# Layer 2's weights by way of copies in DRAM, landed raw in their own places and split later

## The chip, the cores and the metric

The kernel runs on one core of a Trainium2 chip. The metric is the device time of one execution in microseconds. In the text PE is TensorE (PEld its weight loads), DVE VectorE, ACT ScalarE, POOL GpSimd and SP SyncE, which here only issues DMAs.

## The reference

Two cross-attention layers run one after the other over x (16 batches, 256 queries, 320 channels) and a context (16 batches, 256 tokens, 512 channels). H is 20 heads of D = 16.

```python
def layer0(x, ctx):               # 77 text tokens, 179 image tokens
    text, ip = ctx[:, :77], ctx[:, 77:]
    q, k, v = heads(x @ Wq), heads(text @ Wk), heads(text @ Wv)
    text_out = softmax(q k^T * scale) v
    q_sem = softmax(x @ Wq @ (text @ Wk)^T * scale) @ text
    sem   = (q_sem @ ip^T) * scale                      # one for all heads
    ip_probs = softmax(q heads(ip @ Wk_ip)^T * scale + 0.5 * sem) * spatial_mask
    return (text_out + ip_probs heads(ip @ Wv_ip)) @ Wout + bout + x

def layer1(x, ctx):               # 252 text tokens, 4 image tokens
    text, ip = ctx[:, :-4], ctx[:, -4:]
    probs = softmax(q k^T * scale);  text_out = probs v
    sem   = l2norm(probs @ text) @ l2norm(ip)^T         # per head
    ip_probs = softmax(q heads(ip @ Wk_ip)^T * scale + 0.5 * sem) * spatial_mask
    return (text_out + ip_probs heads(ip @ Wv_ip)) @ Wout + bout + x

x = layer0(x, ctx); return layer1(x, ctx)
```

Each layer has six weights: Wq, Wk, Wk_ip, Wv, Wv_ip and Wout. In the kernel those of the first layer are `wq0`, `wk0`, `wki0`, `wv0`, `wvi0`, `wo0`, and those of the second, which the texts call layer 2, `wq1`, `wk1` and so on.

## The kernel before

The work goes in slots, one for four heads of one batch: 80 slots for the first layer (`slot0`), 80 for the second (`slot1`). Within a slot of the first layer `score0` forms the scores of the slot after the next on PE and their maxima on DVE (L676, L677); `maxima0` turns the maxima and ACT sends them as small rows (`qs<-mt`, L687) into Q; `turned0` forms the scores again the other way round (L699), ACT takes the exponential (L702) and POOL multiplies (L705); `attend0` applies the values (L732) and `settle0` transposes and normalizes on DVE (`nt` L743, `tmp` L749). `stacks` loads the K, Q, T (`tph`) and M tiles of the slot four ahead from DRAM by SP.

Everything else is a task with a list of due times in slots: keys, values and queries of coming batches, the closing projection of finished ones, and the preparation of layer 2's weights. `fill(now)` runs what is due at three points of a slot. The order on PE is the order in which the program calls; the other engines' order is set when the program is built, by a planner, except for instructions tied by `queued` (it stands behind the last `anchor` of its engine).

Matrix products run in a format that rounds, so each operand is kept as two halves: `halves` makes the high half by a rounding copy on ACT (L147) and the low half by a subtraction on DVE (L148). A weight's tile holds both, `w[:, 0]` high and `w[:, 1]` low. `in_turn` loads a weight part by part into the two-buffer ring `rawc` and splits each part out of it; a part's load is issued as the part before last is split, and a buffer is taken again only when its split is done. `weights` does this by rows, `weights_by_column` in three column blocks into the `wB` tiles.

Layer 2's weights take the places of layer 1's: `wB` (wki, later wvi), `wA` (wk), `wC` (wv), `wE` (wq), `wF` (wo). The tasks are `weights1` (due from slot 59: the image tokens, their norms, `cip`), `weights7` (from 62: wki, three products for the image keys, wk), `weights6` (from 67: wv, wvi, three products for the image values), `weights2` (from 71.6: wq) and `weights4` (wo; at 2.6 for layer 1, from slot 84 for layer 2). The first keys of layer 2 are due at slot 73.

## Time and profile before

| | |
|---|---|
| median of 3 runs | 1620.4 us (1616.49 to 1623.62) |
| the profiled execution | 1612.52 us |
| its span, first to last instruction | 1610.7 us |
| granted TensorE clock, mean | 0.977 |
| busy share: PE, PEld, DVE, ACT, POOL | 94, 76, 75, 53, 74% |

The profile is of one execution, with each instruction's start and duration. A view of stretches gives each engine's busy time in a piece of the span; a view of waits names the waiting engine and line, and after the arrow what ended the wait, with the sum, the count and the longest. A timeline row has start, duration, engine, line and operation, output and input tiles, and in brackets the idle time of the engine just before, with what ended it.

### The profile page before, as it was taken

What the parts mean: (1) busy time and instruction counts of PE and PEld (TensorE: products, weight loads), DVE (VectorE), ACT (ScalarE), POOL (GpSimd) and SP (SyncE); (2) the same over time, 40 slices, a digit from 0 to 9 for tenths busy, and PEclk for the clock granted to TensorE, in tenths of its full rate; (3) what the DMA queues carried; (4) which work ended last, traced back from release to release, by engine and by line L of the source; (5) the groups of instructions that cost most, each with busy time, mean ns of one, the idle gap of its engine ahead of it and who ended that gap; (6) DMA issues with size and microseconds to landing.
All of it is one profiled execution on the core that took longest, in us unless ns stands there. A gap on an engine that the chain in (4) does not pass through costs nothing.

```text
span 1610.7 us, 36262 instructions
## 1 busy us (share of the span) xinstructions
PE 1518.9 (94%) x13194; PEld 1218.1 (76%) x13194; DVE 1212.2 (75%) x2426; ACT 847.1 (53%) x1861; POOL 1195.7 (74%) x1227
## 2 busy tenths in 40 slices
PE   7899999999999899789999999999999999999996
PEld 6787878787878787577777777777777777777765
DVE  5466777777777678877877787778777887788785
ACT  5344545555555545446656556555655655565562
POOL 3358787878787867777688768876877787778785
PEclk9899999999999899799999999999999999999998
DMA  6767777777677576665424333433343333423301
GB/s 218 214 200 204 206 204 206 205 205 211 199 204 210 170 213 174 162 198 177 149 67 133 114 127 96 131 119 120 96 136 121 107 109 127 130 90 104 110 27 45
DMA packets 235741, 243.05 MB, mean 151 GB/s; under 512 B 19050, under 2 KB 219468, under 8 KB 235564
## 3 DMA queue, kind: packets, MB, share of 16 engines
q1 hardware_dynamic: 233356, 239.44, 49.7%
q8 instruction: 105, 1.72, 0.4%
q10 hardware_dynamic: 2208, 1.30, 0.3%
q14 instruction: 72, 0.59, 0.1%
HBM read 116.78 MB, written 88.18 MB: 127 GB/s over the span
## 4 chain that ended last, share of the span: by engine, by line
PE 63%; DMA 9%; DVE 8%; POOL 8%; ACT 4%; issue 3%; SPq 1%; ACTq 0%; POOLq 0%; DVEq 0%
PE X L205 16%; PE X L839 13%; PE X L551 7%; PE P L732 6%; PE P L848 4%; PE S L675 4%; PE T L798 3%; PE P L851 3%; PE T L699 3%; POOL wt L830 2%; DMA kd<-kst 2%; DMA qs<-qd 2%; DMA qs<-mt 2%; PE S L803 2%; DVE wt L840 1%
## 5 line engine op out<-in xcount | busy, mean ns | idle before, releaser
L705 POOL TENSOR_TENSOR P<-P,rs 128x512 f32<-128x512 f32 x320 | 413.8, 1313 | 149.6 <-ACT P L702 149.5
L830 POOL TENSOR_TENSOR wt<-P,ctb 128x512 f32<-128x512 f32 x320 | 419.0, 1324 | 95.0 <-ACT ctb L829 93.6
L839 PE MATMUL X<-ctb,gm 128*128 128x512 f32 x1120 | 329.9, 412 | 0.7 <-DVE wt L840 0.4
L702 ACT ACTIVATE P<-T 128x512 f32<-128x512 f32 x320 | 176.0, 595 | 211.8 <-PE T L699 113.9
L839 PEld LDWEIGHTS X<-ctb,gm 128*128 128x128 f32 x1120 | 188.9, 188 | 69.2 <-issue 15.2
L840 DVE TENSOR_TENSOR wt<-X,wt 128x512 f32<-128x512 f32 x320 | 218.4, 683 | 18.9 <-PE X L839 13.4
L804 DVE TENSOR_REDUCE mn<-S 128x4 fp32r<-128x1008 f32 x160 | 191.7, 1198 | 49.1 <-PE S L803 48.9
L829 ACT ACTIVATE ctb<-P 128x512 fp32r<-128x512 f32 x320 | 195.1, 630 | 40.1 <-PE X L839 35.8
L811 ACT ACTIVATE P<-T 128x512 f32<-128x512 f32 x320 | 173.1, 593 | 68.9 <-PE P L848 53.8
L677 DVE TENSOR_REDUCE mn<-S 128x4 fp32r<-128x716 f32 x160 | 142.5, 891 | 0.0
L699 PE MATMUL T<-qs,ks 127*128 127x256 f32 x640 | 111.7, 294 | 21.9 <-DVE tmp L749 9.8
L732 PE MATMUL P<-P,vr 128*32 128x256 f32 x1920 | 128.7, 404 | 0.9 <-DVE mx L604 0.9
L675 PE MATMUL S<-ks,qs 125*128 125x256 f32 x640 | 118.4, 309 | 4.9 <-DVE mn L677 2.8
L675 PEld LDWEIGHTS S<-ks,qs 125*128 125x128 f32 x640 | 89.2, 196 | 41.3 <-issue 36.2
L551 PE MATMUL X<-ho,wF 128*128 128x256 f32 x768 | 113.2, 291 | 6.5 <-DVE ho L541 3.0
L551 PE MATMUL X<-hq,wE 128*128 128x256 f32 x768 | 109.7, 286 | 7.1 <-ACT hq L540 3.2
L917 POOL TENSOR_TENSOR r<-u,rs 128x40 f32<-128x40 f32 (+2 forms) x17 | 108.7, 6394 | 7.4 <-DVE u L914 7.2
L551 PEld LDWEIGHTS X<-ho,wF 128*128 128x128 f32 x768 | 103.7, 195 | 12.7 <-DVE ho L541 4.6
L699 PEld LDWEIGHTS T<-qs,ks 127*128 127x128 f32 x640 | 92.5, 197 | 27.2 <-DVE tmp L749 11.2
L551 PEld LDWEIGHTS X<-hq,wE 128*128 128x128 f32 x768 | 102.3, 193 | 11.3 <-ACT hq L540 3.7
L205 PE MATMUL X<-cta,wA 128*128 128x252 f32 (+1 forms) x720 | 101.1, 287 | 8.9 <-ACT wA L147 5.8
L205 PEld LDWEIGHTS X<-cta,wA 128*128 128x128 f32 x720 | 94.3, 193 | 15.1 <-ACT wA L147 6.1
(207 smaller groups left out, 2854.9 us busy)
## 6 DMA issues: line engine op xcount, KB each, us to landing
qd<-q SPq DMA_DIRECT2D x96, 384.0 KB
qs<-tph SPq DMA_DIRECT2D x64, 308.0 KB
kd<-kst SPq DMA_DIRECT2D x73, 256.0 KB
rawc<-in_cT_dram SPq DMA_DIRECT2D x60, 256.0 KB
qs<-qd SPq DMA_DIRECT2D x80, 192.0 KB
ks<-kd SPq DMA_DIRECT2D x80, 192.0 KB
ks<-kd SPq DMA_DIRECT2D x160, 96.0 KB
qs<-qd SPq DMA_DIRECT2D x160, 96.0 KB
```

The source lines that it names most:

```text
L205: last = mm(out, lhs(a, k), rhs(b, k), start=i == 0, stop=i == len(terms) - 1)
L551: mm(pp, w(s, k, slice(m * 128, (m + 1) * 128)), a[:, t], start=i == 0, stop=i == len(terms) - 1)
L675: mm(sp[:, h], Q[: XROW + T0, h, t * 128 : (t + 1) * 128], K[: XROW + T0, h], start=True, stop=True)
L699: mm(st[p][:, j], K[:KS0, 2 * p + j, t * 128 : (t + 1) * 128], Q[:KS0, 2 * p + j], start=True, stop=True)
L702: exp = anchor(nc.scalar.activation(pt, st[p], AF.Exp, scale=SCALE))
L705: anchor(nc.gpsimd.tensor_mul(pt, pt, rs[:, t : t + 1].to_broadcast([128, 2, S])))
L732: mm(pv[32 * s : 32 * s + 32, o : o + S], v[:, vt, h : h + 32], P[k, s // 2][:, t, s % 2], start=vt < 2, stop=vt != 1,)
L804: anchor(nc.vector.tensor_reduce(maxes[k + 2][:, t], sp[:, :, :T1], axis=AX.X, op=ALU.max))
L829: nc.scalar.activation(R[k, u][:, t], P[k, u][:, t], AF.Copy, scale=0.5)
L830: anchor(nc.gpsimd.tensor_sub(W[k, u][:, t], P[k, u][:, t], f(R[k, u][:, t])))
L839: mm(yp, gm[:, gb], R[k, u][:, kt], start=i == 0, stop=i == len(blocks[n]) - 1)
L840: nc.vector.tensor_mul(W[k, u][:, n], yp, W[k, u][:, n])
```

## The change

The 22 row blocks of layer 2's six weights are copied from the inputs into tiles in DRAM (`aside`), one block at a time: every second slot from 14 to 48, and once a slot from 58 to 61. Each copy stands on SP's queue behind the last K load of `stacks0`, which is an anchor now. Later each weight is brought from its copy, unsplit, into the low halves of its own place, in one load (three for the column blocks), as soon as that place's last reader in layer 1 is done: the `LANDINGS`, due at slots 62, 66.6, 68 and 84. The splits then read and write in place: the high half is copied from the low one, and the low half has the high one subtracted from itself. `weights7`, `weights6` and `weights4` start a slot later than before (63, 68, 85); `weights2` stays at 71.6, with one step less. Layer 1's output weight keeps the old way under a name of its own, `first_output`.

```diff
-    def weights(w_d, tag, half=None, wait=0, raw="raw"):
-        ...
-        yield from in_turn([(w_d[k * 128 : (k + 1) * 128], w[:, 0, k], w[:, 1, k]) for k in range(kt)], wait, raw)
+    aside = {}
+
+    def set_aside():
+        for name, w_d in (("wk", wk1_d), ("wv", wv1_d), ("wvi", wvi1_d), ("wq", wq1_d), ("wo", wo1_d), ("wki", wki1_d)):
+            aside[name] = dram.tile(list(w_d.shape), F32, name=f"{name}_aside")
+            for k in range(w_d.shape[0] // 128):
+                rows = slice(k * 128, (k + 1) * 128)
+                queued(nc.sync.dma_start(aside[name][rows], w_d[rows]))
+                yield
+
+    landing = {}
+
+    def land(name, tag):
+        src = aside[name].rearrange("(k p) n -> p k n", p=128)
+        if tag == "wB":
+            parts = landing[name] = [buf("wB", [128, 2, 4, 128], FR, bufs=SIZES["WB"]) for m in range(3)]
+            for m, w in enumerate(parts):
+                queued(nc.sync.dma_start(f(w[:, 1]), src[:, :, m * 128 : (m + 1) * 128]))
+        else:
+            w = landing[name] = buf(tag, [128, 2, src.shape[1], src.shape[2] + (NIP if name == "wv" else 0)], FR)
+            queued(nc.sync.dma_start(f(w[:, 1, :, : src.shape[2]]), src))
+
+    def cast(parts):
+        for hi, lo in parts:
+            halves(hi, lo, f(lo), nc.vector, True)
+            yield
+
+    def weights(name, half=None):
+        w = landing.pop(name)
+        n = w.shape[3] - (NIP if name == "wv" else 0)
+        yield from cast([(w[:, 0, k, :n], w[:, 1, k, :n]) for k in range(w.shape[2])])
...
-    def weights_by_column(w_d, wait=0, raw="raw"):
-        ...
-        yield from in_turn([(src[:, :, m * 128 : (m + 1) * 128], w[:, 0], w[:, 1]) for m, w in enumerate(parts)], wait, raw)
+    def weights_by_column(name):
+        parts = landing.pop(name)
+        yield from cast([(w[:, 0], w[:, 1]) for w in parts])
...
             if part == "K":
-                dma(K[0:XROW], stack_rows(kd[0][b // 2][:, :, b % 2])[:, hs])
+                anchor(nc.sync.dma_start(f(K[0:XROW]), stack_rows(kd[0][b // 2][:, :, b % 2])[:, hs]))
...
+    LANDINGS = (
+        ("wki", "wB", 62, ("k0", B // 2 - 1)),
+        ("wk", "wA", 62, ("k0", B // 2 - 1)),
+        ("wv", "wC", 66.6, ("v0", B - 1)),
+        ("wvi", "wB", 66.6, ("w7",)),
+        ("wq", "wE", 68, ("q0", B - 1)),
+        ("wo", "wF", NS + 4, ("c0", B - 1)),
+    )
...
-    task(("w7",), thirds(13, 62), weights7, ("w1",), ("k0", B // 2 - 1))
-    task(("w6",), thirds(13, 67), weights6, ("w7",), ...)
-    task(("w2",), [71.6, 72, 72.2, 72.6, 73], weights2, ("q0", B - 1), ("w6",))
+    task(("w7",), thirds(13, 63), weights7, ("w1",), ("land", "wki"), ("land", "wk"))
+    task(("w6",), thirds(13, 68), weights6, ("w7",), ("land", "wv"), ("land", "wvi"), ...)
+    task(("w2",), [71.6, 72, 72.2, 72.6], weights2, ("land", "wq"), ("w6",))
...
-    task(("w4", 1), spread(NS + 4, 0.33, 4), lambda: weights4(1), ("c0", B - 1))
+    task(("w4", 0), [2.6, 2.8, 3, 3.2], first_output, ("k0", 1))
+    task(("aside",), [14 + 2 * i for i in range(18)] + [58, 59, 60, 61], set_aside)
+    for name, tag, t, *needs in LANDINGS:
+        task(("land", name), [t], lambda name=name, tag=tag: iter([land(name, tag)]), *needs)
+    task(("w4", 1), [NS + 5, NS + 5.33, NS + 5.67], weights4, ("land", "wo"))
```

More of the change, by code (lines that the diff above doesn't have):

```diff
@@ L168, in in_turn @@
                 yield
-    def weights(w_d, tag, half=None, wait=0, raw="raw"):
-        rows, n = w_d.shape
-        kt = rows // 128
-        w = buf(tag, [128, 2, kt, n], FR)
-        yield from in_turn([(w_d[k * 128 : (k + 1) * 128], w[:, 0, k], w[:, 1, k]) for k in range(kt)], wait, raw)
+    aside = {}
[6 more added lines that the diff above has]
+                yield
@@ L176, in weights @@
+    def cast(parts):
[6 more added lines that the diff above has]
+        yield from cast([(w[:, 0, k, :n], w[:, 1, k, :n]) for k in range(w.shape[2])])
         if half is not None:
             nc.vector.tensor_scalar_mul(w[:, 1, 2], f(w[:, 1, 2]), half)
+        if name == "wv":
+            w1["wv"] = w
         return lambda s, k, m=slice(None): w[:, s, k, m]
-    def weights_by_column(w_d, wait=0, raw="raw"):
-        parts = [buf("wB", [128, 2, 4, 128], FR, bufs=SIZES["WB"]) for m in range(3)]
-        src = w_d.rearrange("(k p) n -> p k n", p=128)
-        yield from in_turn([(src[:, :, m * 128 : (m + 1) * 128], w[:, 0], w[:, 1]) for m, w in enumerate(parts)], wait, raw)
+    def weights_by_column(name):
+        parts = landing.pop(name)
+        yield from cast([(w[:, 0], w[:, 1]) for w in parts])
@@ L185, in weights_by_column, with first_output @@
         return lambda s, k, m: parts[m.start // 128][:, s, k]
+    def first_output():
+        w = buf("wF", [128, 2, 3, CP], FR)
+        yield from in_turn([(wo0_d[k * 128 : (k + 1) * 128], w[:, 0, k], w[:, 1, k]) for k in range(3)], 0.1, "rawc")
+        nc.vector.tensor_scalar_mul(w[:, 1, 2], f(w[:, 1, 2]), tmask[:, 4:5])
+        wo.append(lambda s, k, m=slice(None): w[:, s, k, m])
     def all_halves(jobs, rings):
@@ L401, in weights7 @@
         cip = w1["cip"]
-        wki1 = yield from weights_by_column(wki1_d, 0.3, "rawc")
+        wki1 = yield from weights_by_column("wki")
         for m in range(3):
@@ L407, in weights7 @@
             yield
-        w1["k"] = yield from weights(wk1_d, "wA", None, 0.3, "rawc")
+        w1["k"] = yield from weights("wk")
     def weights6():
         cip = w1["cip"]
-        wv = w1["wv"] = buf("wC", [128, 2, 4, H * D + NIP], FR)
-        parts = [(wv1_d[k * 128 : (k + 1) * 128], wv[:, 0, k, : H * D], wv[:, 1, k, : H * D]) for k in range(4)]
-        yield from in_turn(parts, 0.3, "rawc")
-        wvi1 = yield from weights_by_column(wvi1_d, 0.3, "rawc")
+        w1["v"] = yield from weights("wv")
+        wvi1 = yield from weights_by_column("wvi")
         vip = buf("rawc", [128, 512], bufs=2, name="vip")[:BI, :CP]
@@ L436, in weights2, with weights4 @@
     def weights2():
-        wq.append((yield from weights(wq1_d, "wE", tmask[:, 3:4], 0.3, "rawc")))
-    def weights4(l):
-        wo.append((yield from weights((wo0_d, wo1_d)[l], "wF", tmask[:, 4:5], (0.1, 0.3)[l], "rawc")))
+        wq.append((yield from weights("wq", tmask[:, 3:4])))
+    def weights4():
+        wo.append((yield from weights("wo", tmask[:, 4:5])))
     def weights3():
@@ L1055, in xattn2 @@
     task(("w1",), thirds(7, 59), weights1)
-    task(("w7",), thirds(13, 62), weights7, ("w1",), ("k0", B // 2 - 1))
-    task(("w6",), thirds(13, 67), weights6, ("w7",), *[(x, c) for c in range(B) for x in ("v0", "m0t")])
-    task(("w2",), [71.6, 72, 72.2, 72.6, 73], weights2, ("q0", B - 1), ("w6",))
+    task(("w7",), thirds(13, 63), weights7, ("w1",), ("land", "wki"), ("land", "wk"))
+    task(("w6",), thirds(13, 68), weights6, ("w7",), ("land", "wv"), ("land", "wvi"), *[(x, c) for c in range(B) for x in ("v0", "m0t")])
+    task(("w2",), [71.6, 72, 72.2, 72.6], weights2, ("land", "wq"), ("w6",))
     for i in range(2):
         task(("w3", i), [NS - 4 + 5 * i], weights3)
-    task(("w4", 0), [2.6, 2.8, 3, 3.2], lambda: weights4(0), ("k0", 1))
-    task(("w4", 1), spread(NS + 4, 0.33, 4), lambda: weights4(1), ("c0", B - 1))
+    task(("w4", 0), [2.6, 2.8, 3, 3.2], first_output, ("k0", 1))
[3 more added lines that the diff above has]
+    task(("w4", 1), [NS + 5, NS + 5.33, NS + 5.67], weights4, ("land", "wo"))
     def stacks(k):
```

## The prediction

> **What bounds the kernel now.** I read the page's first two parts, then the busy time by stretches cut at the first exponential of a slot (L702, four to a slot), then the waits of those stretches, and last the order of time on VectorE where PE waits for it.

> ```profile
> PE 1518.9 (94%) x13194; PEld 1218.1 (76%) x13194; DVE 1212.2 (75%) x2426; ACT 847.1 (53%) x1861; POOL 1195.7 (74%) x1227
> PE   7899999999999899789999999999999999999996
> PEclk9899999999999899799999999999999999999998
> DMA  6767777777677576665424333433343333423301
> q1 hardware_dynamic: 233356, 239.44, 49.7%
> q8 instruction: 105, 1.72, 0.4%
> ```

> PE is busy 94% of the span and the kernel follows it. A slice is 40.3 us; PE falls under 9 tenths, apart from start and end, only in slices 13, 16 and 17 (523 to 725 us), where the layers overlap and layer 2's weights are brought in. There alone can this change win.

> ```profile
> core 0: us, PE busy (x) PEld busy (x) DVE busy (x) ACT busy (x) POOL busy (x), PEclk, DMA share, GB/s
> 428.90:509.10 80.20, 76.83 (x722) 66.34 (x721) 60.43 (x135) 40.66 (x94) 65.38 (x64) 1.00 0.72 206
> 541.10:554.80 13.70, 7.66 (x68) 6.41 (x67) 8.56 (x25) 5.92 (x11) 10.25 (x10) 0.80 0.85 248
> 581.90:602.20 20.30, 18.16 (x174) 15.72 (x172) 14.29 (x37) 8.46 (x23) 11.95 (x11) 1.00 0.83 240
> 602.20:633.50 31.30, 31.30 (x298) 27.62 (x298) 26.42 (x54) 18.01 (x40) 26.58 (x23) 1.00 0.54 148
> 633.50:643.20 9.70, 6.66 (x60) 5.22 (x58) 7.25 (x14) 3.58 (x9) 5.77 (x6) 0.91 0.81 231
> 643.20:658.20 15.00, 7.66 (x48) 5.29 (x48) 11.54 (x27) 5.11 (x13) 6.81 (x9) 0.61 0.64 178
> 658.20:680.70 22.50, 18.03 (x174) 13.56 (x173) 18.27 (x36) 11.48 (x22) 19.03 (x18) 0.88 0.57 145
> ```

> Rows 2 to 7 are slots 58, 62 to 63, 64 to 67, 68, 69 and 70 to 72; row 1 is ten steady slots of layer 1. Length less PE's busy time is PE's idle time: 3.4 us in the ten steady slots, then 6.0, 2.1, 0, 3.0, 7.3 and 4.5. Slot 58 waits for the image tokens, which the change leaves alone. Slots 68 to 72 together lose 14.9 us in 47.2, and in them the granted clock is low as well.

> **Where the raw loads are late.** The waits of slots 63, 68, 69 and 70 to 72, in this order:

> ```profile
> ACT wB L147 <- DMA rawc<-in_wki_dram: 4.8, 1, 4.8
> PE X L551 <- DVE M L365: 1.7, 1, 1.7
> ACT wC L147 <- DMA rawc<-in_wv_dram: 3.9, 1, 3.9
> DVE wC L148 <- ACT wC L147: 2.4, 1, 2.4
> PE X L683 <- DVE mn L677: 2.8, 1, 2.8
> PE T L699 <- DVE tmp L749: 3.9, 1, 3.9
> PE X L616 <- DVE sp L612: 3.5, 1, 3.5
> ACT wB L147 <- DMA rawc<-in_wvi_dram: 2.7, 1, 2.7
> PE X L683 <- DVE mn L677: 2.2, 2, 2.0
> PE X L683 <- DMA qs<-tph: 1.3, 1, 1.3
> SPq L82 <- DMA rawc<-in_wvi_dram: 4.8, 1, 4.8
> ```

> Three times ScalarE stands before a split whose raw weights have not landed: 4.8, 3.9 and 2.7 us. What PE pays is less. The 4.8 us cost it nothing: slots 64 to 67 have no idle time. The 1.7 us in slot 63 came of two splits on VectorE ahead of the token part that PE wanted. In slot 68 the chain is whole:

> ```profile
> 636.24 0.44 DVE L777 SCALAR_TENSOR_TENSOR xc<-X,bo,xc 128x256 f32<-128x256 f32 x1
> 639.13 0.49 DVE L148 TENSOR_TENSOR wC<-rawc,wC 128x320 fp32r<-128x320 f32 x1 [2.45 <-ACT wC L147]
> 639.54 0.71 DVE L743 STREAM_TRANSPOSE nt<-P 128x512 f32<-128x512 f32 x1
> 640.54 0.88 DVE L677 TENSOR_REDUCE mn<-S 128x4 fp32r<-128x716 f32 x1
> 641.50 2.35 DVE L529 TENSOR_TENSOR kb<-kip,kmask 128x384 fp32r<-128x384 f32 x2
> 644.24 1.45 DVE L148 TENSOR_TENSOR wC<-rawc,wC 128x320 fp32r<-128x320 f32 x1
> 646.71 0.41 DVE L749 TENSOR_TENSOR tmp<-nt,P 128x256 f32<-128x256 f32 x1
> 653.03 1.59 DVE L148 TENSOR_TENSOR wB<-rawc,wB 128x512 fp32r<-128x512 f32 x1
> 654.71 1.09 DVE L612 TENSOR_SCALAR sp<-sp,mx 128x77 f32<-128x77 f32 x1
> ```

> VectorE stands 2.45 us for the cast that stands for in_wv; the row maxima behind it are late, and PE waits 2.8. The next wait, 3.9 us for tmp, is the backlog: VectorE is still late when the two kb products and a split come ahead of tmp. The 3.5 us are for sp, with a 1.59 us split ahead of it in VectorE's order.

> **The change part by part.**

> The splits stay: 20 casts and 20 subtractions as before, in place, so that their engines' time is as before: 0.

> The gain, wait by wait. Slot 63: in the new order of VectorE the token part stands ahead of the first split, and the loads of all three wki parts are issued a slot before it: −1.7 (least 0). Slot 68: wv is issued at 66.6 for a split at 68.2; the 2.45 us wait goes and PE's 2.8 with it: −2.8. Slot 69: tmp inherits 2.4 us less of backlog, and sp now stands ahead of the wB splits (1.59): −4.0 of 7.4; the kb products and one wC split stay ahead of tmp. Slots 70 to 72: SP no longer stands 4.8 us for in_wvi's buffer with the stack loads behind it, so that the 1.3 goes, and of the 2.2 for mn I take 0.7: −2.0. Sum −10.5.

> Against it stands VectorE's own work. In 633.5 to 680.7 it is busy 7.25 + 11.54 + 18.27 = 37.1 us of 47.2; in the densest stretch above it reached 26.42 of 31.30, 84%. At 84%, 37.1 us need 44.1, which would leave only 3.1 us to be won there, 4.8 with slot 63. Two wC splits move into these slots besides. I take the middle of 10.5 and 4.8: −7.5.

> The copies: 22 transfers of 192 KB or 160 KB from DRAM to DRAM (18 in slots 14 to 48, 4 in slots 58 to 61), each behind a K stack load and its Q load in SP's queue, in 16 rows of up to 12 KB, one for each DMA engine. No such transfer is in this trace. From the page, q8 moved 1.72 MB in 105 packets in 0.4% of 16 engines' span: 0.004 x 16 x 1610.7 / 105 = 0.98 us for 16.4 KB, so 0.74 us for 12 KB; q1's rate, 239.44 MB in 49.7%, gives 0.66. If the read and the write of DRAM don't overlap it is twice that, 1.5. The engines can carry it: two steady slots are 16 us at a share of 0.72, so 4.5 us are free and a copy takes 0.7. What may not carry it is what lies closest to PE there:

> ```profile
> PE T L699 <- DMA qs<-mt: 8.5, 13, 0.8
> ACT P L702 <- DMA kd<-kst: 16.7, 4, 4.3
> L82 SPq DMA_DIRECT2D rawc<-in_wk_dram x4: 358/363/452, 592.6 to 613.2; - x4
> L148 DVE TENSOR_TENSOR wB<-rawc,wB x6: 677/794/1751, 589.0 to 662.3; 128x512 fp32r<-128x512 f32 x6
> ```

> Between 160 and 540 us, some 46 slots, PE waited 13 times for the small rows of maxima (mt) that ScalarE sends into Q; there is no slack in those 13. A copy in front of them costs up to its own 0.7: with all 22 hit 15 to 16 us, with 13 in 46 of them 22 x 0.28 x 0.7 = 4.3, with none 0. The copy is issued at the end of a slot, with the Q load ahead of it still moving, and the rows go out in the next; most miss each other. I take +1.5. SP's issue, 0.36 us each, comes to 8 us spread over some 450.

> The landings: ten loads for twenty, the same bytes, but in bursts: wki and wk, 1.57 MB, at slot 62; wv and wvi, 1.44 MB, at 66.6; wq, 0.59 MB, at 68; wo at 84. In the program as built, the DMAs of SP and ScalarE take eight semaphores in turn, and each waits for the one eight before it. So the fourth maxima row of slot 62 now waits, on ScalarE, for the second wB landing, with the slot's last two exponentials queued behind it; the M load for slot 66 waits on SP for wA, with that slot's K and Q loads behind it. At 240 GB/s for a share of 0.83, a full share is 289 GB/s and 1.57 MB take 5.4 us; those loads have a slot more than that slot's end, 8.0 us in the steady row. ScalarE stood at this place before too, for kd (four such waits between 160 and 540 took 16.7 us and left PE 3.4 idle in ten slots), so I take 0, with −1 to +4 as the bounds. The splits that start one slot later (wki 63, wv 68) still end before slot 73, where layer 2's keys begin: 0.

> If the clock recovers, more is won; I leave that to a rival. Sum: −7.5 + 1.5 + 0 = −6.0. The profiled execution took 1612.5 us (span 1610.7), 7.9 under the median of the three runs; it would become 1606.5, and on the median 1620.4 − 6.0 = 1614.4.

> **The rivals.**

> The clock comes back too. The clock in slot 69 is 0.61 and in 70 to 72 0.88. At full clock PE's 7.66 and 18.03 us of work would be 4.7 and 15.9: 5.2 us on top of the whole 10.5, so −15.7 and 1604.7. For it: the two waits of slot 69, 3.9 and 3.5 us, are the ones that the change shortens. Against it: VectorE's 84%. [...]

> The copies reach PE (the slow side). If a copy keeps its engine for 1.5 us and the maxima rows of its slot are behind it in half the cases, 22 x 1.5 x 0.5 = 16.5, less 7.5 won: +9.0 and 1629.4; it turns the sign from 7.5 us in all, 0.34 us a copy. For it: the 13 waits without slack, a DMA share of 0.72 in the very slots used. Against it: 3.4 us of PE idle in ten such slots although ScalarE stood 4.3 us at a time. [...]

> The wait moves. ScalarE stands at the wB landing instead of at in_wki, and in slots 68 to 72 VectorE's order alone keeps PE waiting; with −1.7 for slot 63 and +1.5 for the copies this is 1620.2. The same comes if the change doesn't do what it says: where a landing is later than its split, the old wait stands at the new name.

> **How the numbers follow.** Forecast 0.40, clock 0.24, copies 0.16, moved wait 0.20. About 0.5% (8.1 us) is what a measurement of this kernel can tell from no change: below 1612.3, above 1628.5. Faster: 0.22 of the clock case and 0.12 of the forecast, 0.34. Slower: 0.11 of the copies and 0.05 of the moved wait with a bad landing (+4) and copies at 4 or more, 0.16. Same: 0.50. Down to 1603 some 0.08 are left out, above 1628 some 0.12 (the clock's overshoot, and copies at their dearest). The forecast with the bounds of its own terms is 1608 to 1620.

> **What would show it.** Right: no wait of ScalarE for a weight's DMA in slots 63 to 72; PE idle under 9 us in slots 68 to 72 in place of 14.9; slots 14 to 48 as long as before. The clock case: a granted clock near 1 in slot 69. The copies: more and longer PE waits for mt between 160 and 540 us, and ten steady slots above 81 us. The moved wait: ScalarE idle for wB's or wC's landing, PE idle as before. I would be wrong in the gain if VectorE's order kept all of 14.9 us, and wrong in the cost if the ten steady slots grew by over 1 us.

## The result, and the profile after

| | median | runs |
| --- | --- | --- |
| before | 1617.7 us | 12, 1614.7 to 1623.6 |
| after | 1626.7 us | 12, 1623.7 to 1635.1 |

The ratio is 1.0058, with a 95% interval of 1.0041 to 1.0076: slower by 0.58%, some 9 us, where 6 us less had been forecast. The profiled execution of the changed kernel has a span of 1624.5 us (before 1610.7).

The page of the changed kernel, first three parts: busy time, slices, queues.

```profile
PE 1529.4 (94%) x13194; PEld 1223.9 (75%) x13194; DVE 1206.3 (74%) x2426; ACT 848.2 (52%) x1861; POOL 1195.4 (74%) x1227
PE   7899999999999899689999999999999999999996
PEclk9799999999999999889999999999999999999998
q1 hardware_dynamic: 233900, 243.64, 50.3%
```

PE's busy time has grown by 10.5 us for the same 13194 matmuls: of the 13.8 us that the span has grown, most shows not as idle time but as matmuls at a lower granted clock (mean 0.972 for 0.977). The queues carry 4.2 MB more, the copies, in 0.6 points more of the engines' time.

Busy time by stretches of the changed kernel, cut at the same slots as before: ten steady slots (44 to 53), slot 58, 62 to 63, 64 to 67, 68, 69, 70 to 72.

```profile
core 0: us, PE busy (x) PEld busy (x) DVE busy (x) ACT busy (x) POOL busy (x), PEclk, DMA share, GB/s
437.30:518.90 81.60, 78.76 (x724) 67.17 (x723) 59.36 (x135) 40.73 (x94) 65.91 (x64) 0.98 0.73 210
551.00:563.90 12.90, 7.46 (x68) 6.36 (x67) 8.75 (x25) 5.97 (x11) 10.27 (x10) 0.89 0.92 272
590.40:608.30 17.90, 15.73 (x137) 12.39 (x135) 10.78 (x21) 7.12 (x17) 9.53 (x9) 0.90 0.94 285
608.30:646.50 38.20, 37.06 (x337) 32.36 (x337) 31.03 (x72) 18.87 (x46) 29.34 (x27) 1.00 0.60 164
646.50:653.30 6.80, 5.85 (x58) 4.48 (x56) 5.63 (x12) 3.47 (x9) 4.22 (x4) 1.00 0.98 287
653.30:667.00 13.70, 9.20 (x72) 5.54 (x72) 11.19 (x26) 5.71 (x15) 8.64 (x9) 0.75 0.80 215
667.00:690.60 23.60, 16.70 (x148) 12.31 (x149) 17.89 (x35) 11.14 (x23) 17.11 (x17) 0.86 0.32 78
```

Length less PE's busy time: slots 68 and 69 lose 1.0 and 4.5 us where they lost 3.0 and 7.3; slots 70 to 72 lose 6.9 where they lost 4.5. Slots 62 to 67 hold work that moved between them (174 matmuls in slots 62 and 63 before, 137 now); together they went from 51.6 to 56.1 us. The steady slots took 80.2 and take 81.6, at a clock of 0.98 in place of 1.00. A second profile of the kernel before, taken later, has 54.0 us in slots 62 to 67 and 81.0 in the steady slots, so that some half of these two differences is the kernel's own spread.

Its waits in slots 62 and 63 (three rows), in slot 69, in slots 70 to 72 (two rows), and in 160 to 550 us (three rows):

```profile
ACT P L737 <- DMA wB<-wki_aside: 4.9, 1, 4.9
ACT P L737 <- DMA qs<-mt: 3.9, 1, 3.9
PE T L734 <- DMA qs<-mt: 2.2, 3, 0.9
PE X L651 <- DVE sp L647: 2.7, 1, 2.7
PE X L718 <- DVE mn L712: 3.3, 3, 1.4
PE X L586 <- DVE ho L576: 3.0, 1, 3.0
ACT P L737 <- DMA qs<-mt: 16.4, 4, 5.9
PE T L734 <- DMA qs<-mt: 9.5, 13, 1.2
ACT P L737 <- DMA kd<-kst: 8.7, 2, 4.5
```

No split waits for its weight any more. In slot 62 two exponentials stand 4.9 us, and the row names a wB landing, which they don't read. ScalarE's order of time shows what stands ahead of them, three maxima rows (mt):

```profile
590.66 1.09 ACT L737 ACTIVATE P<-T 128x512 f32<-128x512 f32 x2 [0.65 <-PE T L734]
593.00 3.51 ACTq L722 DMA_DIRECT2D qs<-mt  x3
596.62 1.08 ACT L737 ACTIVATE P<-T 128x512 f32<-128x512 f32 x2 [4.87 <-DMA wB<-wki_aside]
```

By the semaphore events of this trace the three went out at 593.00, 594.44 and 595.95, each within 0.03 us of a landing on its own semaphore: of the M load at 592.98, of the Q load at 594.41 and of the second wB part at 595.93. So the wB landing held ScalarE for 0.9 of the 4.9 us, and two stack loads for 1.2 and 0.8. In layer 1's slots 16.4 us of exponentials are late behind maxima rows, a row of waits that the profile of before does not have between 160 and 540 us; their wait for kd went from 16.7 us to 8.7. The wait for ho in slot 72 is new as well. VectorE's order of time there, after (four rows) and before (two):

```profile
677.73 0.94 DVE L148 TENSOR_TENSOR wE<-wE 128x384 fp32r<-128x384 f32 x1
678.59 0.41 DVE L784 TENSOR_TENSOR tmp<-nt,P 128x256 f32<-128x256 f32 x1
680.12 0.54 DVE L148 TENSOR_TENSOR wE<-wE 128x384 fp32r<-128x384 f32 x1
680.58 1.75 DVE L576 TENSOR_TENSOR ho<-hT,ho 128x512 fp32r<-128x512 f32 x1
```

```profile
670.68 0.69 DVE L541 TENSOR_TENSOR ho<-hT,ho 128x512 fp32r<-128x512 f32 x1
672.81 1.56 DVE L148 TENSOR_TENSOR wE<-rawc,wE 128x384 fp32r<-128x384 f32 x1
```

Two of the wE splits now stand ahead of the ho product that PE wants; before, the ho product came first.

### The profile page after: what moved, and what is told of

Read it like the earlier page. It is cut to its first block, busy times and chain, and to the rows that moved or that the text cites. A ratio compares the mean times of both kernels' runs of the same rounds, so it can differ in the third digit from the quotient of the medians.

```text
span 1624.5 us, 36244 instructions
## 1 busy us (share of the span) xinstructions
PE 1529.4 (94%) x13194; PEld 1223.9 (75%) x13194; DVE 1206.3 (74%) x2426; ACT 848.2 (52%) x1861; POOL 1195.4 (74%) x1227
## 3 DMA queue, kind: packets, MB, share of 16 engines
q8 instruction: 105, 1.72, 0.5%
## 4 chain that ended last, share of the span: by engine, by line
PE 42%; POOL 7%; DVE 5%; ACT 2%; issue 2%; DMA 1%; SPq 0%; POOLq 0%; DVEq 0%; ACTq 0%
PE X L874 13%; PE X L242 9%; PE X L586 4%; PE P L883 4%; PE T L833 3%; PE P L886 3%; POOL wt L865 2%; PE S L838 2%; DVE wt L875 1%; DVE mn L839 1%; POOL cta L148 1%; POOL hq L576 1%; PE X L537 1%; POOL r L952 1%; PE P L767 1%
## 5 line engine op out<-in xcount | busy, mean ns | idle before, releaser
L734 PE MATMUL T<-qs,ks 127*128 127x256 f32 x640 | 113.8, 295 | 26.8 <-DMA qs<-mt 15.9
L586 PEld LDWEIGHTS X<-ho,wF 128*128 128x128 f32 x768 | 101.5, 191 | 15.3 <-DVE ho L576 8.0
L242 PE MATMUL X<-cta,wA 128*128 128x252 f32 (+1 forms) x720 | 104.9, 293 | 8.5 <-ACT wA L147 6.2
L242 PEld LDWEIGHTS X<-cta,wA 128*128 128x128 f32 x720 | 98.0, 199 | 15.2 <-ACT wA L147 6.4
```

What stands on the lines that cost most here:

```text
L242: last = mm(out, lhs(a, k), rhs(b, k), start=i == 0, stop=i == len(terms) - 1)
L586: mm(pp, w(s, k, slice(m * 128, (m + 1) * 128)), a[:, t], start=i == 0, stop=i == len(terms) - 1)
L734: mm(st[p][:, j], K[:KS0, 2 * p + j, t * 128 : (t + 1) * 128], Q[:KS0, 2 * p + j], start=True, stop=True)
```

## The experiments

All ratios are against the kernel before in the same comparison. In e1_tiny, e1_none and e2_ho the landings read layer 1's stored keys, so that layer 2 computes with those in place of its weights. The table holds lengths in us, from the busy time by stretches of each profile, cut at the first exponential of a slot; the kernel before was profiled twice.

| kernel | ratio (95%) | slots 20–49 | 62–67 | 68–71 | 72–77 |
| --- | --- | --- | --- | --- | --- |
| before, two profiles | 1 | 241.1, 242.4 | 51.6, 54.0 | 38.1, 37.9 | 54.2, 54.8 |
| after | 1.0058 (1.0041–1.0076) | 248.8 | 56.0 | 32.1 | 61.4 |
| e1_tiny | 1.0042 (1.0024–1.0061) | 245.3 | 57.3 | 32.4 | 59.5 |
| e1_none | 1.0021 (1.0006–1.0037) | 242.6 | 56.3 | 31.1 | 62.1 |
| e1_copies_only | 1.0059 (1.0037–1.0082) | 250.0 | 50.7 | 33.5 | 64.5 |
| e1_twice | 1.0079 (1.0053–1.0105) | 255.7 | 57.3 | 31.6 | 58.2 |
| e2_four | 1.0370 (1.0334–1.0407) | 287.6 | 56.4 | 33.8 | 63.2 |
| e2_four_narrow | 1.0390 (1.0351–1.0428) | 281.6 | 55.9 | 33.8 | 66.4 |
| e2_four_tiny | 1.0359 (1.0323–1.0395) | 290.2 | 54.8 | 33.5 | 64.0 |
| e3_eight_tiny | 1.0427 (1.0393–1.0460) | 282.6 | 62.5 | 33.9 | 59.3 |
| e3_four_pool | 1.0420 (1.0386–1.0454) | 294.3 | 55.9 | 33.1 | 57.6 |
| e3_pool_ho | 1.0082 (1.0057–1.0108) | 247.3 | 59.3 | 30.5 | 62.8 |
| e4_four_own | 1.0092 (1.0065–1.0118) | 253.1 | 53.2 | 32.7 | 63.6 |
| e5_own_tiny | 1.0085 (1.0061–1.0108) | 249.2 | 51.9 | 32.8 | 64.4 |
| e5_own_narrow | 1.0094 (1.0073–1.0115) | 252.7 | 51.1 | 33.1 | 63.5 |
| e2_ho | 0.9992 (0.9970–1.0014) | 243.6 | 58.1 | 30.4 | 57.3 |
| e4_after_own | 1.0046 (1.0027–1.0065) | 244.9 | 56.9 | 31.7 | 61.4 |
| e4_after_own_ho | 1.0026 (1.0008–1.0044) | 246.5 | 56.5 | 33.5 | 54.7 |
| e5_values | 1.0007 (0.9991–1.0024) | 245.2 | 54.8 | 30.8 | 62.3 |

**Copies or landings, bytes or place.** Four kernels.

e1_tiny, the copies at 64 bytes (the last line is shortened at the dots):

```
-                queued(nc.sync.dma_start(aside[name][rows], w_d[rows]))
+                queued(nc.sync.dma_start(aside[name][k : k + 1, :16], w_d[k * 128 : k * 128 + 1, :16]))
-        src = aside[name].rearrange("(k p) n -> p k n", p=128)
+        src = kd[0][0].rearrange("s r b t -> (s r b t)")[...].rearrange("(k p n) -> p k n", p=128, n=...)
```

> The 22 copies are cut to 64 bytes each, and the landings read as many bytes from layer 1's stored keys in DRAM, so that layer 2 computes with those in place of its weights; every instruction of every engine stands where it stands in the changed kernel, with the same eight semaphores in the same turn. Theory A (the copies' bytes: packets of 10 to 12 KB hold the DMA engines, rows for PE come late, and the clock drops after the longer waits): the +8 to +10 us of slots 14 to 58 go, ten steady slots take 80 to 81 us, the median is 1616 to 1620. Theory B (the copies' places in SP's queue and in the turn of the semaphores, or the new order of the engines): bytes don't matter, ten steady slots stay at 82 to 83.5 us and the median at 1625 to 1628.

e1_none, the landings of e1_tiny and no copies:

```
-    task(("aside",), [14 + 2 * i for i in range(18)] + [58, 59, 60, 61], set_aside)
```

> No copies at all; the landings read as many bytes from layer 1's stored keys in DRAM in place of layer 2's weights. With the copies gone the planner orders VectorE, ScalarE and GpSimd a little differently in slots 14 to 61. Theory A (bytes): as the run with 64-byte copies, 1616 to 1620, since only the bytes cost. Theory B (queue places, turn of the semaphores, order): only here the loss goes, 1616 to 1620, and the run with 64-byte copies is 6 us or more longer than this one. Either way what stands against the kernel before, 1617.7, is the landings' own worth: my prediction gave them -7.5, so 1610; the profile of the changed kernel (slots 58 to 72 won 3 us, 72 to 90 lost 8) says +1 to +5, so 1619 to 1622.

e1_copies_only, the kernel before with the task ("aside",), set_aside and the anchor on the K loads added:

> The kernel before with its own loads of layer 2's weights, and the 22 copies beside them at the same slots, read by nobody. Theory A (bytes): 18 copies cost 8 to 10 us by slot 58 and the median is 1625 to 1628, ten steady slots at 82 to 83.5 us. Theory B (order or semaphore turn as it fell in the changed kernel): the cost would be other here, 1618 to 1622. The rival that the loss comes from the landings alone: 1617 to 1619.

e1_twice, in set_aside of the changed kernel, behind each copy:

```
+                queued(nc.sync.dma_start(again[rows], w_d[rows]))
```

> The changed kernel with each copy made twice, one behind the other, into two places. Theory A (bytes): twice the cost in slots 14 to 58, 8 to 10 us more than the changed kernel, 1635 to 1637. Theory B (place and order): 1625 to 1630, since the second copy stands at the same place.

Measured: 1626.1, 1621.2, 1628.9 and 1630.6 us. The copies alone, unread, slow the old kernel by all that the change does (0.59%). Without copies the landings still cost 0.21% where a gain of 0.5% had been forecast. The 64-byte copies' median lies in theory B's range; by the ratio, and by the 245.3 us of slots 20 to 49, they lie between the kernel without copies and the changed one. Doubling the bytes cost a fifth of a per cent in place of the half that theory A wanted, though slots 20 to 49 grew by 6.9 us. In e1_none and e1_twice the planner's order also differs a little from the changed kernel's. At one copy a place the comparison is too weak to tell bytes from place.

**Four copies at a place, to make the effect large.** In the kernel with unread copies, where `four` holds four tiles for each weight:

```
-                queued(nc.sync.dma_start(aside[name][rows], w_d[rows]))
+                [queued(nc.sync.dma_start(x[rows], w_d[rows])) for x in four]                        # e2_four
+                [queued(nc.sync.dma_start(x[rows, : w_d.shape[1]], w_d[rows])) for x in four]        # e2_four_narrow, rows of x 16 elements longer
+                [queued(nc.sync.dma_start(x[k : k + 1, :16], w_d[k * 128 : k * 128 + 1, :16])) for x in four]   # e2_four_tiny
```

> The kernel before with its own weight loads, and at each of the 22 places four copies of the same 128 rows into four places in DRAM, read by nobody (12 KB rows as in the changed kernel). In the runs so far one copy at each place cost 0.59% (9.5 us), and doubling the changed kernel's copies 0.21% more in the median, 0.46 us a copy in slots 20 to 50 of the profile. Theory A (bytes): 66 copies more at 0.3 to 0.46 us, 1647 to 1658. Theory B (place in the queue, turn of the semaphores): the cost does not grow with the bytes, 1625 to 1632, and equal to the run with four 64-byte copies.

> As the run with four copies at each place, the same bytes and the same order of every engine, but the target's rows are 16 elements longer than the copy, so that a transfer is 128 rows of 1.5 KB (1.25 KB for wv) in place of 16 rows of 12 KB. Theory A1 (a long packet keeps its engine from the small rows that PE waits for): at most half of the cost of the 12 KB rows, 1630 to 1640. Theory A2 (the engines' time as such, whatever the packet): as with 12 KB rows or more, 1645 to 1665. Theory B: 1625 to 1632.

> As the run with four copies at each place, with the same order of every engine and the same turn of the semaphores, but 64 bytes each. Theory A (bytes): near the kernel before, 1618 to 1624. Theory B (place, SP's issue time, turn of the semaphores): all of the cost remains, 1626 to 1632 or, if each issue adds, up to 1640.

Measured: 1678.0, 1680.3 and 1679.3 us. All three lie above every range that either theory had named: neither foresaw the size. But the three are alike. Their traces have the same order of instructions on every engine and of the DMAs of SP and ScalarE (e2_four_narrow but for two swaps among VectorE's first 30); they differ in what 88 DMAs move, 16.8 MB in rows of 12 KB, the same in rows of 1.5 KB, or 5.6 KB in all. They cost the same 3.6 to 3.9%. Theory A falls, for the bytes and for the length of the packets. Where the time goes shows in the kernel with four 64-byte copies, in the order of time of ScalarE (first five rows), VectorE and PE, slot 20:

```profile
243.82 0.36 ACT L696 CAST mt<-X 8x256 fp32r<-8x256 f32 x1
246.93 0.57 ACTq L698 DMA_DIRECT2D qs<-mt  x1
247.60 1.08 ACT L713 ACTIVATE P<-T 128x512 f32<-128x512 f32 x2 [3.42 <-PE P L743]
250.07 0.57 ACTq L698 DMA_DIRECT2D qs<-mt  x1
250.68 0.29 ACT L147 CAST kst<-X 128x154 fp32r<-128x154 f32 x1 [2.00 <-DMA ks<-M]
251.00 0.32 DVE L148 TENSOR_TENSOR kst<-X,kst 128x154 fp32r<-128x154 f32 x1 [5.07 <-ACT kst L147]
252.23 0.89 DVE L688 TENSOR_REDUCE mn<-S 128x4 fp32r<-128x716 f32 x1
253.26 1.19 PE L710 MATMUL T<-qs,ks 127*128 127x256 f32 x4 [5.21 <-DVE mn L688]
```

The row of maxima is ready at 244.18, and ScalarE issues its first DMA at 246.93. A later one goes out at 250.07, 1.4 us after the exponentials ahead of it have ended; the row of the kst cast behind it names what ScalarE stood for, the M load. For the cast VectorE stands 5.07 us, the row maxima behind that are late, and PE waits 5.21 us. ScalarE waits here for no data of its own: it waits for the semaphore of the DMA eight before, its partner in the turn that the program as built gives to SP's and ScalarE's DMAs (in the trace of the changed kernel SP's 1121 and ScalarE's 472 count on the same eight semaphores). By the semaphore events the partner of the first is a 64-byte copy, issued at 241.92 and landed at 246.85, and that of the later one the M load, landed at 250.05: both rows go out within 0.1 us of that. Every DMA put between moves the partner one nearer. Counted in the program as built, of the 148 maxima rows issued in slots 16 to 52 those whose partner is a load or store of the slot that they stand in are 10 before, 17 with one copy at a place, 28 with two, 32 with four. That is theory T.

The count alone doesn't follow the cost: two copies at a place cost 0.79% (e1_twice, landings included), four 3.70%, for 28 and 32 rows. The time stood shows more. The same semaphore events tell for each DMA of ScalarE and SP whether it went out just as its partner landed, with the engine free over 0.1 us before. In slots 20 to 49:

| | ScalarE: times, us stood | SP: times, us stood |
| --- | --- | --- |
| before, two profiles | 24, 24.3; 22, 22.9 | 7, 4.6; 3, 2.8 |
| one copy: changed kernel; e1_copies_only | 28, 28.8; 28, 32.7 | 10, 6.4; 11, 8.6 |
| four: e2_four; e2_four_tiny | 41, 48.8; 40, 48.7 | 18, 16.4; 22, 22.9 |
| eight: e3_eight_tiny | 43, 57.6 | 37, 37.2 |

**The turn, or SP's issue time.** e3_eight_tiny is e2_four_tiny with range(8) for range(4); e3_four_pool (e2_four) and e3_pool_ho (the changed kernel, with the wE times of e2_ho below) issue the copies by GpSimd (`four` there, the one copy in e3_pool_ho):

```
+                [queued(nc.gpsimd.dma_start(x[rows], w_d[rows]), anchors[mybir.EngineType.SP]) for x in four]
```

> The kernel before with eight copies of 64 bytes at each place, issued by SP. Theory T (turn of the semaphores): what counts is how many maxima rows wait for a load of their own slot; in the program as built, of 148 rows in slots 16 to 52 that is 10 before, 17 with one copy at each place, 28 with two, 32 with four and 38 with eight, so that eight cost little more than four, 1680 to 1700. Theory I (SP's issue time, some 0.4 us a DMA, makes the stack loads late): the cost grows with the number, twice that of four, 1730 to 1745.

> The kernel before with the four full copies (192 KB or 160 KB each) at each of the 22 places, but issued by GpSimd, whose DMAs take eight semaphores of their own. Four copies issued by SP cost 3.6 to 3.9% whether they moved 192 KB or 64 bytes each (1678, 1680 and 1679 us). Theory T (the turn: DMAs of SP and ScalarE share eight semaphores in turn, each waits for the one eight before it, and every transfer put between makes ScalarE's maxima rows wait for younger loads): the bytes stay and the cost goes, 1618 to 1632, the upper part if GpSimd's own issue time (some 1 us each beside its 74% busy) tells. Theory A (bytes): 1660 or more.

> The changed kernel with its 22 copies issued by GpSimd in place of SP, and the wE splits at 72, 72.2 and 72.6. Theory T with the ho wait: the changed kernel's 1626.7 less 5 for the turn (the run without copies) and 3 for the ho product ahead of the splits, 1616 to 1620, no slower than the kernel before; up to 1622 if GpSimd's issues delay the products it shares with ScalarE. If the bytes of the copies cost after all, 1622 to 1626.

Measured: 1687.4, 1686.2 and 1631.9 us. Eight DMAs at a place cost 0.7 points more than four, not twice as much, so that SP's issue time falls as the main cause. The two runs through GpSimd missed: 4.2% and 0.8% slower, and by its forecast e3_four_pool would speak for theory A. The 64-byte copies of e2_four_tiny stand against that, and another cost is in sight, though no run isolates it: with the copies' issues (0.49 us each in the trace of e3_four_pool, by the rows of wk and wv; the 1 us of its forecast was an estimate that no run shows) GpSimd was busy for 221.7 us in slots 20 to 49 (197.8 before), VectorE for 202.1 (178.9), and in 190 to 490 us the first waits of PE are for ho, which ScalarE and VectorE make of what GpSimd wrote:

```profile
PE X L562 <- ACT ho L551: 13.7, 4, 4.4
PE X L562 <- DVE ho L552: 10.6, 3, 5.7
```

**Only the turn taken away.** The copies stay in SP's queue and count on a semaphore of their own (their targets are plain tensors in DRAM here, no longer tiles of the framework):

```
+    def own(inst):
+        tc.no_tile_sem_insts.add(inst.ins.name)
+        return inst.then_inc(own_sem, 16)
-                [queued(nc.sync.dma_start(x[rows], w_d[rows])) for x in four]
+                [own(queued(nc.sync.dma_start(x[rows], w_d[rows]))) for x in four]
```

> The run with four full copies at each place (1678.0 us), with one thing changed: the copies' DMAs count on a semaphore of their own, outside the eight that SP's and ScalarE's other DMAs take in turn. The order of VectorE, ScalarE and GpSimd, SP's issues, the bytes are the same; the copies still stand in SP's queue. In the program as built 10 of 148 maxima rows in slots 16 to 52 wait for a load of their own slot, as before the change, in place of 32. Theory T (the turn): nearly all of the 60 us goes, 1618 to 1630. Theory O (the order that the planner chose): 1670 to 1685. Theory A (bytes) and I (SP's issue time): 1670 to 1685 too.

> The run with four copies at each place outside the turn (1631.4 us, +0.92%), the copies cut to 64 bytes; the order of VectorE, ScalarE and GpSimd and SP's issues stay. If the rest is the copies' bytes (88 at 0.16 us): 1617 to 1621. If it is SP's issues or the planner's order: 1628 to 1634.

> The same run with full copies in rows of 1.5 KB (1.25 KB for wv) in place of 12 KB. If long packets keep the engines from the small rows: below the 12 KB rows' 1631, 1620 to 1626. If it is the engines' time as such: 1629 to 1636. If bytes don't count: as the run with 64 bytes.

Measured: 1631.4, 1632.9 and 1631.8 us, the first just above theory T's 1618 to 1630. The traces of e2_four and e4_four_own have the same order on every engine and of the DMAs of SP and ScalarE, and the bytes are the same; 47 of the 60 us are gone, and ScalarE's and SP's standing in slots 20 to 49 is back at 22.7 and 0.9 us. So the turn is shown as the cause of some three quarters of what four copies cost. The rest, 0.85 to 0.94%, is again the same for 64 bytes, 1.5 KB rows and 12 KB rows; SP's issues and the planner's order, which isn't that of the kernel before, are both left for it, and these runs don't part the two. In the profiles it stands in slots 20 to 49 (7 to 12 us) and, where no copy is left, in 72 to 77 (9 us), less 5 us won in 68 to 71. Busy time by stretches in slots 20 to 49, e2_four and then e4_four_own:

```profile
239.28:526.86 287.58, 250.88 (x2176) 213.62 (x2178) 188.35 (x403) 121.78 (x282) 196.71 (x189) 0.93 0.71 212
```

```profile
237.74:490.85 253.11, 235.52 (x2162) 201.99 (x2162) 180.82 (x403) 123.05 (x282) 198.16 (x189) 0.98 0.81 241
```

Of the 34.5 us between them 19.1 are idle time of PE (36.7 against 17.6) and 15.4 its busy time, with the clock at 0.93 against 0.98. e4_four_own carries the higher DMA share, 0.81, at little cost.

**The changed kernel without the turn, and without the wait for ho.** e2_ho is e1_none, and e4_after_own_ho is e4_after_own, with

```
-    task(("w2",), [71.6, 72, 72.2, 72.6], weights2, ("land", "wq"), ("w6",))
+    task(("w2",), [72, 72.2, 72.6, 73], weights2, ("land", "wq"), ("w6",))
```

e4_after_own counts the copies by own() as above, each landing waiting for all 22; in its trace PE, VectorE, ScalarE and GpSimd keep the order of the changed kernel.

> The kernel without copies (landings read layer 1's stored keys, 1621.2 us), with the times of the three wE splits at 72, 72.2 and 72.6 as they were before the change, in place of 71.6, 72 and 72.2; VectorE then takes the ho product of the slot ahead of the splits that stood in front of it. Theory (the landings' loss is this one wait): the 2.8 to 3.0 us that PE waits for ho in slot 72 shrink to 1 or less, and with the clock that follows it 1616 to 1618.5. Rival (VectorE's backlog is only passed on, as in slots 68 to 77 it was in every run so far): idle time of slots 72 to 78 stays at 12 to 13 us, 1620 to 1622.

> The changed kernel whole, with its 22 copies counted on a semaphore of their own; the ten landings wait for all 22 by that semaphore. The order of VectorE, ScalarE and GpSimd is that of the changed kernel. Theory T: the 5 us between the changed kernel (1626.7) and the run without copies (1621.2) go, 1619 to 1623. Theory O: 1625 to 1628.

> As the run before it, with the wE splits at 72, 72.2 and 72.6. Theory T with the ho wait: 1616 to 1620, the kernel before's time (1617.5 to 1619.5 in the runs so far) within 0.2%: the landings' gain in slots 68 to 72 is paid back elsewhere even so. Theory O: 1622 to 1625.

> The kernel before, for a second profile. Slots 20 to 50 take 240 to 243 us as in the first one (241.0). If slots 62 to 78 took 143.9 us there by luck of the clock, they take 146 to 149 here, as in the run that only adds unread copies (148.6); if 143.9 is typical, the landings lose 4 to 6 us there.

Measured: 1618.0, 1624.9, 1621.3 and 1617.1 us. The times of the wE splits are worth 0.29 points in one pair and 0.20 in the other, 3 to 5 us; in each pair the two intervals overlap, but both go the same way. PE's wait for ho fell only from 2.8 us to 1.7 and from 3.0 to 1.2, so it is not the whole of this. The turn at one copy a place is worth 0.12 points by the medians, less than their intervals can part. In slots 20 to 49 the profile goes from 248.8 to 244.9 us, half of the way to before, and ScalarE's standing from 28.8 to 24.5, that of before: the waits are shown, their price in the changed kernel is not. e4_after_own thus lands above its forecast, and what is left of it over e1_none (0.25 points) isn't explained.

The second profile of before took 146.7 us in slots 62 to 77 where the first took 143.9, so that by the forecast the first was lucky, by 2.4 us in slots 62 to 67. The 54 us in slots 72 to 77 came again and are typical, and the 57 to 66 us there of every other kernel but e4_after_own_ho are a loss; e1_copies_only has it (64.5) with no landing at all. Nor can the short slots 68 to 71 be put down to the landings alone: with the old loads and unread copies they take 32.7 to 33.9 us too, where before took 38. Slots 68 to 77 together, from one profile each:

| | 62–67 | 68–77 |
| --- | --- | --- |
| before, two profiles | 51.6, 54.0 | 92.3, 92.8 |
| old loads: e1_copies_only; e4_four_own | 50.7; 53.2 | 98.0; 96.4 |
| landings: changed kernel; e1_none | 56.0; 56.3 | 93.5; 93.2 |
| landings, wE later: e2_ho; e4_after_own_ho | 58.1; 56.5 | 87.7; 88.2 |

With the wE times of before, e2_ho and e4_after_own_ho take 4 to 5 us less than the kernel before in slots 68 to 77, and 2.5 to 6.5 us more in slots 62 to 67. The groups are not clean: e3_pool_ho, with landings and these wE times, has 93.4 in slots 68 to 77, and e3_eight_tiny and e3_four_pool, with the old loads, 93.1 and 90.7. Why unread copies shift time from slots 68 to 71 into 72 to 77 stays open.

**Where the landings pay.** Only wv and wvi land (8 copies, outside the turn), their splits a slot later as in the changed kernel, the rest as before.

> Only wv and wvi by copies (8, every fourth slot from 14, outside the turn) and landings at 66.6, with the value weights' splits a slot later as in the changed kernel; wki, wk, wq and wo loaded and split as in the kernel before. If the landings' gain is that of slots 68 to 72 (the changed kernel won 5 to 6 us there) and the loss came with wki and wk at slot 62 and with the wE splits: 1612 to 1616, faster than the kernel before (1617.5). If whatever is won in slots 68 to 72 is paid back in 72 to 78: 1617 to 1620.

Measured: 1619.8 us, no different from before. Slots 68 to 71 took 30.8 us in place of 38, and 72 to 77 took 62.3 in place of 54: what is won is paid back, and slots 68 to 77 take 93.1 us, as before. No kernel of this study is faster than the one before.

## Why the prediction was wrong

Three terms of the sum missed: the gain was put too high, the copies too low, and the earlier wE splits had no price. By ratios the change sums to 6.0 us for the copies (after against e1_none; forecast 1.5), 4.7 for the wE splits (e1_none against e2_ho; forecast 0) and −1.3 for the landings (e2_ho against before; forecast −7.5): 9.4 us. Each is uncertain by some 4 us, so none of the three is shown to be the largest miss.

**The copies, +1.5: the wrong mechanism.** They cost 9.5 us alone and 6.0 within the change (1.0058 against 1.0021). The bounds, 0 to 16, held it; the value was chosen by a wrong mechanism. The term was a packet time, 0.7 us, times the chance that a row of maxima lies behind it. The packets came as worked out, 16 of 12 KB for a copy of 192 KB, at a median of 0.54 us, but with 88 copies 64 bytes cost as much as 192 KB: packet time shows no cost here. What mattered there were the two figures set aside beside it: the turn of eight semaphores, which the prediction worked out for the landings alone and not for the 22 DMAs that the copies add to the same turn, and SP's issues with the order that the planner makes of them. With four copies at a place the turn is shown as three quarters of the cost. With one, as in the change, its waits are in the traces, but of the 0.37 points it accounts for 0.12 by the medians, inside the noise; the rest stays open.

**The rival that the copies reach PE** gave +9.0 us, which is what was measured. That is luck: its 16.5 us for the copies were 0.75 us each (measured 0.27 within the change, 0.43 alone), its 7.5 us of gain did not come, and the cause was another, since 88 copies of 64 bytes are as slow as 88 of 192 KB. Nor did the length of the rows tell: those of 1.5 KB and of 12 KB came out alike twice (1680.3 and 1678.0; 1631.8 and 1631.4 us). That a copy keeps its engine for 1.5 us no run shows; a packet of 12 KB took 0.54.

**The gain, −7.5: idle time taken for time won.** The waits went as worked out: ScalarE's three are gone, slot 68 lost 1.0 in place of 3.0, tmp is no longer waited for in slot 69, sp went from 3.5 to 2.7. But PE's idle time in slots 68 to 72 fell from 14.9 to 12.4, not under 9, and slots 62 to 67 (2 to 4 us longer) and 72 to 77 (7 longer) took it back. Nor is less idle time less time. PE is the bottleneck, and the sum held the length of its matmuls fixed. Busy time by stretches of slots 62 to 67, 68 to 71 and 72 to 77, before and then e2_ho:

```profile
581.86:633.46 51.60, 49.46 (x469) 43.34 (x468) 40.70 (x89) 26.47 (x63) 38.49 (x34) 1.00 0.65 185
633.46:671.57 38.11, 26.42 (x230) 19.61 (x229) 28.01 (x60) 15.89 (x36) 22.52 (x25) 0.78 0.65 174
671.57:725.80 54.23, 44.09 (x406) 36.84 (x405) 42.56 (x86) 24.34 (x53) 44.65 (x47) 0.97 0.67 194
```

```profile
583.67:641.76 58.09, 54.46 (x472) 45.12 (x471) 41.44 (x92) 26.13 (x61) 39.07 (x35) 0.94 0.67 194
641.76:672.12 30.36, 25.86 (x227) 18.84 (x225) 25.18 (x56) 16.00 (x38) 23.59 (x24) 0.78 0.67 185
672.12:729.45 57.33, 47.68 (x404) 38.46 (x403) 43.01 (x86) 24.46 (x54) 43.32 (x46) 0.91 0.60 173
```

In e2_ho, the landings without copies and with the wE splits at their old times, PE's idle time in these slots falls from 24.0 us (25.4 in the second profile of before) to 17.8, near what was forecast. Its busy time, for two matmuls fewer, rises from 120.0 (121.3) to 128.0, at clocks of 0.94, 0.78 and 0.91 where before had 1.00, 0.78 and 0.97. In the changed kernel the idle time hardly falls (23.3 us) and the busy time rises all the same (126.3); e4_after_own_ho goes the way of e2_ho, by less (20.7 idle, 124.0 busy). The lower clock goes with most of the 7 to 8 us in e2_ho: length times the clock not granted is 10.0 us in the three rows of before and 15.3 in those of e2_ho. Why the clock is lower with less idle time isn't shown. The clock case had the clock rise with the shorter waits, and no case had it fall. VectorE's own work, weighed at a gain of 4.8, came nearer in size; no run tests it as the cause.

**The splits, 0.** "The splits that start one slot later … still end before slot 73" looked at their end, not at their place in VectorE's order. The wE splits start at 71.6, earlier than before, and two of them stand ahead of ho: PE waits 3.0 us for it, and the median loses 3 to 5 us by these times.

**The landings in bursts, 0 (−1 to +4).** The place was right to the row: in slot 62 a maxima row waited for the second wB landing with the slot's last two exponentials queued behind it. Of ScalarE's 4.9 us there that landing made 0.9, the stack loads in the same turn the rest with the issues. The 2 to 4 us of slots 62 to 67 lie within the bounds; in e2_ho it is 4 to 6.5.

**The signs named beforehand.** No ScalarE wait for weights: right of the splits, wrong of the maxima row of slot 62. Idle time under 9: wrong. Slots 14 to 48 as long as before: wrong, by 6 to 8 us in slots 20 to 49. The ten steady slots are 1.4 us longer than in the first profile of before and 0.6 longer than in the second, too close to decide. PE's waits for mt are 13 as before, 9.5 us in place of 8.5. The clock case: 0.75 in slot 69 for 0.61, but the clock was lost again in layer 1's slots (0.98 in the ten steady ones for 1.00) and in 72 to 77 (0.86 for 0.97).

## What to carry to other kernels

Four copies at a place cost 3.70% in the turn of completion semaphores and 0.92% outside it, and 64 bytes cost as much as 192 KB (3.59% in the turn, 0.85% outside). So, in a program whose DMAs share such a turn, count an added DMA by its place there before counting its bytes: ask which DMA each following one now waits for, on which engine, and what stands behind it in that engine's order. In the kernel before, 77 of the 148 maxima rows in slots 16 to 52 have a maxima row as their partner; with four copies at a place 55 have, and the others have a load, a store or a copy. When a step's effect is too small to part two causes, multiply it with the order of the engines held, and take the causes away one by one; what that shows of the large effect must still be weighed for the small one. And where the bottleneck engine's clock differs between runs, idle time taken from it is not yet time won: in slots 62 to 77 of e2_ho 6.2 us less idle time of PE came with 8.0 us more busy time, so look at its busy time for the same work as well.

## What the runs showed of the hardware

**16.8 MB that cost nothing here.** 16.8 MB of copies from DRAM to DRAM, at a DMA share of 0.81 in slots 20 to 49 in place of 0.71, cost no more than 88 DMAs of 64 bytes (e4_four_own and e5_own_tiny: 1631.4 and 1632.9 us, both outside the turn).

```profile
304.72:308.13 3.41, 3.41 (x42) 2.79 (x34) 2.44 (x6) 0.01 (x1) 3.41 (x4) 1.00 1.03 308
308.13:311.54 3.41, 1.59 (x11) 1.02 (x8) 3.29 (x13) 2.12 (x6) 3.18 (x3) 1.00 0.98 333
311.54:314.96 3.42, 3.42 (x22) 3.02 (x26) 1.23 (x4) 2.18 (x7) 3.42 (x5) 0.54 0.93 227
314.96:318.37 3.41, 3.41 (x39) 2.64 (x32) 3.29 (x6) 1.28 (x3) 1.78 (x3) 0.97 1.02 284
```

PE is idle for 1.8 us of the second window, and the whole third one, in which PE never stops, runs at half clock (0.54 and not 0.50 because the cuts lie 0.24 us ahead of the clock's steps): 22 matmuls begin in it, where 42 and 39 begin in the full ones beside it and 27 to 43 in other full windows close by in which PE never stops. In the 20 traces of this case the windows at full clock that were followed by a half one had PE idle for 29 to 100% of their time (median 59%), those followed by a full one for at most 52%. So idle time of 1.0 to 1.8 us within one window came ahead of half clock at times, and not always: 226 windows with as much were followed by a full one. A window at half clock can cost up to 1.7 us of work, an estimate from half of 3.41. The prediction priced waits of 1 to 2 us at their own length.
